# A four-layer graph network: L0's table in a written order with gathers ahead of its branch, and its one-hot columns on ScalarE

## Chip, cores and metric

One core of a Trainium2 chip runs the whole program in one launch. The metric is device time in microseconds (us), the median over runs. The engines are PE (TensorE: matmuls and transposes), DVE (VectorE), ACT (ScalarE), POOL (GpSimd, which issues the indirect DMAs) and SP (SyncE, which issues most other DMAs). Each engine works through its own queue of instructions in order and waits on semaphores that the others raise.

## What is computed

The input is a graph of 6250 nodes with 256 features and 100 000 edges sorted by destination. Four layers follow each other, each as `x = x + layer(relu(layernorm(x)))`. Only the first, L0, is touched; the part of it that matters is:

```python
h = jnp.maximum(_layernorm(x, axis=-1), 0.0)
Qh = (h @ Wq + bq).reshape(N, 8, 32)
Kh = (h @ Wk + bk).reshape(N, 8, 32)
Vh = (h @ Wv + bv).reshape(N, 8, 32)
s = jnp.einsum('nhc,nhc->nh', Qh, Kh) / jnp.sqrt(32.)
alpha = jax.nn.leaky_relu(s[src] + s[dst], 0.2)      # edges and self loops
e = jnp.exp(alpha - segment_max(alpha, dst)[dst])
a = e / segment_sum(e, dst)[dst]
attn = segment_sum(Vh[src] * a[:, :, None], dst).reshape(N, 256)
...
```

After it come a projection, a batch norm, a feed-forward part of width 512 and a second batch norm. L1 is a filter convolution, L2 an attention with edge features, L3 a graph convolution.

## The kernel before

The nodes are padded to 6272, which is NB = 49 blocks of 128. The edges are cut into G = 98 groups of J x 128 = 1024; since they are sorted by destination, the edges of one group reach at most 128 neighbouring nodes, a window that starts 64 nodes further on for each group.

**The table (L187 to L229).** For every block of nodes the kernel normalises the rows (`norm_stats`, `norm_t`), turns them with TensorE, multiplies them with Wq and Wk (into the buffer `ps_Q`) and with Wv (into `ps_V`), and forms the node's score per head on VectorE (L221 to L224). Bias terms of the score are folded into eight more columns of Wv (L194 to L206). A row of 265 numbers, which are V, the 8 scores and a one, is put together (L226 to L228) and stored to the table `vt` in DRAM by SP (L229). The order on each engine in this part is found by a scheduler from priorities; it is not written by hand. The x rows come by seven loads of seven blocks each, all issued by ScalarE at the start (L84 to L89).

**The checks and the branch (L232 to L271).** `first` (an iota on POOL) is the first node of each group's window. `rel` is each edge's destination within it. Minimum and maximum of `rel`, and a bound on the logits, become one flag, which every engine loads: a branch chooses between the fast path described here and a general one, which is not taken with these inputs.

**The edge loop of L0 (L755 to L791)** has its order written by hand, group by group. For group g:

- POOL gathers 8 x 128 rows of `vt` by `src` into one of six ring buffers in `xbuf` (L131, called at L765). A ring buffer comes free when the sums of the group six earlier are done.
- SP loads `drow`, the destinations of group g+2, to all partitions (L686, three buffers), and for a finished block b its own rows `v` (L769).
- `one_hot_t` (L692) makes the one-hot matrix `to` of group g+1 with nodes on partitions. VectorE compares `drow` with `place`, the node number of each partition in group g's window (an iota on POOL, L679). `to` has two buffers.
- `of_dst` (L706): 16 small products fetch each edge's destination score with `to`; `logits0` adds source and destination score and takes the exponential twice on ScalarE (L717 into `ps_E`, L718 into the gathered rows), and VectorE weights the rows (L780).
- `sum_window` (L630): eight products with `oh`, the one-hot matrix with edges on partitions (L698), sum the rows by destination. ScalarE copies the sums out (L632).
- Every second group a block of nodes is complete: `sum_block` (L640), `attn0` (L724 to L729), `turn0` (L735, L737), `project0` (L743) and `residual0` (L751, L753).

In the loop's text `logits0(g)` stands ahead of `one_hot_t(g + 1)`. The two matrices and the loop's order are these lines:

```python
nc.vector.tensor_scalar(tos[g], drows[g], place[:, g:g + 1], None, OP.is_equal)   # L692
...
nc.scalar.activation(ex, al, AF.Exp)                                              # L717
nc.scalar.activation(vg[:, :, D:D + H], al, AF.Exp)                               # L718
...
ex = logits0(g)                                                                   # L777
one_hot_t(g + 1)                                                                  # L778
```

Of the kernel before, what the change touches and what calls it, by code (L numbers as in the profile page):

```python
# [10 lines left out]
F32 = mybir.dt.float32  # L11
I32 = mybir.dt.int32
AF = mybir.ActivationFunctionType
# [22 lines left out]
def tile_gnn(ctx: ExitStack, tc: tile.TileContext, a: dict, out: bass.AP, N: int):  # L36
# [46 lines left out]

    def load_x():  # L84
        for b0 in range(0, NB, 7):
            b1 = min(NB, b0 + 7)
            nc.scalar.dma_start(x[:, b0:b1, :], xv[:, b0:b1, :])

    load_x()  # L89
    src_i = keep.tile([P, GJ], I32, name="src_i")  # L90
# [87 lines left out]

    vt = dram.tile([NP, VR], F32, name="vt")
    sct = dram.tile([NP, 2 * H], F32, name="sct")  # L180
    with ExitStack() as l0:
# [3 lines left out]
        wqk = wp.tile([P, 2, 2 * D], F32, name="wqk")  # L185
        wv = wp.tile([P, 2, D + H], F32, name="wv")
        nc.sync.dma_start(wqk[:, :, 0:D], a["L0_gnn_Wq"].rearrange("(c p) n -> p c n", p=P))  # L187
        nc.sync.dma_start(wqk[:, :, D:2 * D], a["L0_gnn_Wk"].rearrange("(c p) n -> p c n", p=P))
        nc.sync.dma_start(wv[:, :, 0:D], a["L0_gnn_Wv"].rearrange("(c p) n -> p c n", p=P))
        bq, bk = on_all(wp, "L0_gnn_bq", D), on_all(wp, "L0_gnn_bk", D)  # L190
        nc.sync.dma_start(src_i, a["src"])
        nc.sync.dma_start(dst_i, a["dst"])
        isq = 1.0 / math.sqrt(HD)
        nc.vector.tensor_scalar(wqk[:, :, 0:D], wqk[:, :, 0:D], isq, None, OP.mult)  # L194
        nc.vector.tensor_scalar(bq, bq, isq, None, OP.mult)
        both = wp.tile([P, 2, D], F32, name="both")
        other = wp.tile([P, 2, D], F32, name="other")
        nc.vector.tensor_tensor(both, wqk[:, :, 0:D], bk[:, None, :].to_broadcast([P, 2, D]), OP.mult)
        nc.vector.tensor_tensor(other, wqk[:, :, D:2 * D], bq[:, None, :].to_broadcast([P, 2, D]), OP.mult)
        nc.vector.tensor_tensor(both, both, other, OP.add)  # L200
        for k in range(2):
            nc.vector.tensor_reduce(wv[:, k, D:D + H], both[:, k, :].rearrange("p (h c) -> p h c", c=HD),
                                    AX.X, OP.add)
        bqk = wp.tile([P, H, 1], F32, name="bqk")
        nc.vector.tensor_tensor(bq, bq, bk, OP.mult)
        nc.vector.tensor_reduce(bqk[:, :, 0], bq.rearrange("p (h c) -> p h c", c=HD), AX.X, OP.add)  # L206

        with tc.tile_pool(name="a0", bufs=2) as ap:
            for b in range(NB):
                if b % 7 == 0:  # L210
                    norm_stats(b, min(NB, b + 7))
                hb = ht[:, :, b * P:(b + 1) * P]
                norm_t(ps, "T", ap, b, hb)
                qk, v = ps("Q", [P, 2 * D]), ps("V", [P, D + H])
                for k in range(2):
                    nc.tensor.matmul(qk, hb[:, k, :], wqk[:, k, :], start=k == 0, stop=k == 1)  # L216
                    nc.tensor.matmul(v, hb[:, k, :], wv[:, k, :], start=k == 0, stop=k == 1)
                q = ap.tile([P, D], F32, name="q")
                nc.scalar.activation(q, qk[:, 0:D], AF.Copy)
                qq = ap.tile([P, H, HD + 1], F32, name="qq")  # L220
                nc.vector.tensor_tensor(qq[:, :, 0:HD], q.rearrange("p (h c) -> p h c", c=HD),  # L221
                                        qk[:, D:2 * D].rearrange("p (h c) -> p h c", c=HD), OP.mult)
                nc.vector.tensor_tensor(qq[:, :, HD:HD + 1], bqk, v[:, D:D + H][:, :, None], OP.add)
                nc.vector.tensor_reduce(sv[:, b, :], qq, AX.X, OP.add)  # L224
                row = ap.tile([P, VR], F32, name="row", bufs=3)
                nc.scalar.activation(row[:, 0:D], v[:, 0:D], AF.Copy)  # L226
                nc.gpsimd.tensor_copy(row[:, D:D + H], sv[:, b, :])
                nc.gpsimd.memset(row[:, D + H:VR], 1.0)  # L228
                nc.sync.dma_start(vt[b * P:(b + 1) * P, :], row)  # L229


        bad = small.tile([P, 4], F32, name="bad")  # L232
        with tc.tile_pool(name="prep", bufs=1) as prep:
            first = prep.tile([P, G, J], F32, name="first")
            nc.gpsimd.iota(first, pattern=[[HW, G], [0, J]], base=-OFF, channel_multiplier=0,
                           allow_small_or_imprecise_dtypes=True)
            nc.vector.tensor_copy(rel, dst_i)
            rel3 = rel.rearrange("p (g j) -> p g j", j=J)
            nc.vector.tensor_tensor(rel3, rel3, first, OP.subtract)
            nc.vector.tensor_reduce(bad[:, 0:1], rel, AX.X, OP.min)  # L240
            nc.vector.tensor_scalar(bad[:, 0:1], bad[:, 0:1], -1.0, None, OP.mult)
            nc.vector.tensor_reduce(bad[:, 1:2], rel, AX.X, OP.max)
            nc.vector.tensor_scalar(bad[:, 1:2], bad[:, 1:2], P - 1.0, None, OP.subtract)

# [360 lines left out]
    def fast():  # L605
# [43 lines left out]


        l0 = fctx.enter_context(ExitStack())
# [6 lines left out]
        w1, w2 = next(of1), next(of2)  # L658
        NV = 2 * NACC // (J * VR)
        vgs = [xbuf[:, i * J * VR:(i + 1) * J * VR].rearrange("p (j r) -> p j r", j=J) for i in range(NV)]  # L660
        with tc.tile_pool(name="e0", bufs=2) as ep:

            scw = ep.tile([P, NB, 2, 2 * H], F32, name="scw", bufs=1)
            for odd in range(2):
                for b0, b1 in ((0, 32), (32, NB)):
                    t = ps("AB"[odd], [P, b1 - b0, 2 * H])
                    if odd:
                        b2 = min(b1, NB - 1)
                        nc.tensor.matmul(t, shift_by(-OFF), sc[:, b0:b1, :], start=True, stop=False)
                        nc.tensor.matmul(t[:, 0:b2 - b0, :], shift_by(P - OFF), sc[:, b0 + 1:b2 + 1, :],  # L670
                                         start=False, stop=True)
                    else:
                        b2 = max(b0, 1)
                        nc.tensor.matmul(t, shift_by(OFF), sc[:, b0:b1, :], start=True, stop=False)
                        nc.tensor.matmul(t[:, b2 - b0:, :], shift_by(OFF - P), sc[:, b2 - 1:b1 - 1, :],
                                         start=False, stop=True)
                    nc.vector.tensor_copy(scw[:, b0:b1, odd, :], t)
            place = ep.tile([P, G], F32, name="place", bufs=1)
            nc.gpsimd.iota(place, pattern=[[HW, G]], base=-OFF, channel_multiplier=1,  # L679
                           allow_small_or_imprecise_dtypes=True)  # L680
# [7 lines left out]
            def one_hot_t(g):  # L688

                if g < G:  # L690
                    tos[g] = ep.tile([P, J * P], F32, name="to")
                    nc.vector.tensor_scalar(tos[g], drows[g], place[:, g:g + 1], None, OP.is_equal)  # L692

# [15 lines left out]
            def logits0(g):  # L709

                vg, dg = vgs[g % NV], dgs[g]
                al = ep.tile([P, J, H], F32, name="al")
# [42 lines left out]
            with tc.manual_schedule():  # L755
# [5 lines left out]
                for g in range(G + 2):  # L761
                    vg = vgs[g % NV]
                    if g < G:
                        for j in range(J):
                            gather(vg[:, j, :], vt, src_i[:, g * J:(g + 1) * J], j)  # L765
                    loads0(g + 2)
# [8 lines left out]
                    projected = [(b, project0(b)) for b in blocks_done(g - 2)]  # L775
                    if g < G:
                        ex = logits0(g)  # L777
                        one_hot_t(g + 1)  # L778
                        vals = vg[:, :, 0:D].rearrange("p j (h c) -> p j h c", c=HD)
                        nc.vector.tensor_tensor(vals, vals, ex[:, :, :, None].to_broadcast([P, J, H, HD]),  # L780
                                                OP.mult)
# [14 lines left out]
        with tc.tile_pool(name="f0", bufs=2) as fp, Psum("psf", A=3, B=3, T=2) as ps:  # L796
            load_x()
            ff = l0.enter_context(tc.tile_pool(name="ff", bufs=1, side="right"))
# [328 lines left out]
    def slow():  # L1127
# [126 lines left out]
        with tc.tile_pool(name="f0", bufs=1) as fp:  # L1254
# [6 lines left out]
            for b in range(NB):  # L1261
# [7 lines left out]
                for o in range(2):  # L1269
# [6 lines left out]
                    nc.vector.bn_stats(st1[:, o, b, :], ht[:, o, b * P:b * P + n])  # L1276
            load_x()
            rs, sh = feed_forward(wp, fp, ps, w0, st1)
# [189 lines left out]
```

## Time and profile before

| | |
|---|---|
| median of three runs | 5322.65 us (5315.94 to 5338.24) |
| profiled execution: own time, span | 5275.56 us, 5273.8 us |
| mean granted TensorE clock | 0.747 |
| PE, PEld busy | 59%, 46% of the span |
| DVE, ACT, POOL busy | 39%, 11%, 58% |
| DMA traffic | 536.82 MB, mean 102 GB/s |

The first stages within the span, as the instructions' start times show them: L0's table to about 182 us, the checks and the branch to 193 us (first gather at 193.05), L0's edge loop to about 1394 us, L0's feed-forward part to about 1550 us. L1 follows to about 2730, L2 to about 4000 and L3 to the end.

How busy the engines are in the stages that the change touches, from the view of windows (start and end; length; busy time and instructions of PE, PEld, DVE, ACT and POOL; granted clock; DMA share; GB/s):

```profile
0.00:182.00 182.00, 146.93 (x490) 85.44 (x491) 83.38 (x315) 54.17 (x155) 15.40 (x109) 1.00 0.25 82
182.00:192.00 10.00, 0.86 (x3) 0.29 (x3) 8.15 (x19) 0.38 (x1) 2.10 (x2) 0.66 0.04 14
193.00:358.00 165.00, 95.93 (x364) 77.68 (x363) 58.67 (x157) 11.44 (x30) 101.42 (x105) 0.65 0.51 147
358.00:1347.00 989.00, 785.56 (x3457) 660.85 (x3455) 533.66 (x1472) 75.26 (x294) 657.84 (x672) 0.79 0.49 143
```

A row of the instruction groups reads: line, engine, operation, what it writes and reads, how often; its busy time in us and the mean of one in ns; the idle time of its engine just before it, and what ended most of that. In the waits view the numbers are us in total, times, and the longest. "remote" and "issue" stand for waits whose end the records do not explain by an instruction of this core, and for time in which the engine waited for nothing that the profile shows.

### The profile page before, as it was taken

How to read it: one execution, taken by the hardware profiler on the slowest of the kernel's cores; microseconds unless marked ns; L12 is line 12 of the kernel's file. 1: busy time of each engine (PE TensorE's matmuls, PEld its weight loads, DVE VectorE, ACT ScalarE, POOL GpSimd, SP SyncE). 2: the span in 40 equal slices, each digit the busy share in tenths (PEclk: the TensorE clock that was granted, in tenths of full speed). 3: DMA queues.
4: the chain of work that ended last, by engine and by line, in shares of the span. 5: the costliest groups of instructions: out<-in, count | busy, mean ns of one | idle time of the engine just before them, and what ended most of it. 6: DMA issues, size and time to landing. Idle time of an engine off the chain costs nothing.

```text
span 5273.8 us, 42603 instructions
## 1 busy us (share of the span) xinstructions
PE 3126.5 (59%) x12132; PEld 2420.0 (46%) x12133; DVE 2067.2 (39%) x6350; ACT 601.7 (11%) x1517; POOL 3046.8 (58%) x3261
## 2 busy tenths in 40 slices
PE   7577878778895154544544545555555355554645
PEld 4366766667545143333333434444444244443434
DVE  4355555555525155555555523233333122222212
ACT  2100000000133000000000012222222100000000
POOL 0456666666104665565665266666666466666665
PEclk9778777787897577677667777777777677776777
DMA  2344544445302233333333233333333233333332
GB/s 96 115 127 143 149 140 143 140 142 149 97 0 63 60 99 97 103 103 96 98 100 100 76 98 99 98 99 99 101 100 100 74 93 102 97 98 98 98 98 84
DMA packets 258746, 536.82 MB, mean 102 GB/s; under 512 B 65096, under 2 KB 144966, under 8 KB 258502
## 3 DMA queue, kind: packets, MB, share of 16 engines
q0 software_dynamic: 137984, 364.28, 25.8%
q1 hardware_dynamic: 107750, 156.85, 9.4%
q10 hardware_dynamic: 12768, 12.85, 0.8%
q8 instruction: 104, 1.70, 0.1%
q14 instruction: 140, 1.15, 0.1%
HBM read 504.57 MB, written 29.15 MB: 101 GB/s over the span
## 4 chain that ended last, share of the span: by engine, by line
PE 35%; another core or an unknown queue 26%; issue 16%; DVE 11%; ACT 5%; POOL 4%; DMA 1%; DVEq 0%; SPq 0%; ACTq 0%; POOLq 0%
PE ps_S L630 12%; PE ps_S L1118 5%; POOL vg L131 4%; PE ps_A L706 4%; DVE oh L932 3%; PE ps_T L640 3%; DVE big L969 2%; PE ps_Q L216 2%; PE ps_A L401 2%; PE ps_B L407 2%; DVE ea L974 2%; PE ps_B L743 1%; DVE te L975 1%; PE ps_S L972 1%
## 5 line engine op out<-in xcount | busy, mean ns | idle before, releaser
L131 POOL DMA_INDIRECT vg<-xt,src_i x1568 | 1490.6, 951 | 870.7 <-issue 542.2
L131 POOL DMA_INDIRECT big<-ht,src_i x784 | 742.0, 946 | 475.2 <-PE ps_S L972 215.9
L131 POOL DMA_INDIRECT xbuf<-vt,src_i x784 | 767.5, 979 | 397.6 <-issue 180.4
L630 PE MATMUL ps_S<-vg,oh 128*128 128x258 f32 x1568 | 476.0, 470 | 467.6 <-DVE oh L1039 455.5
L630 PEld LDWEIGHTS ps_S<-vg,oh 128*128 128x128 f32 x1568 | 373.7, 242 | 554.1 <-DVE oh L1039 467.4
L640 PE MATMUL ps_T<-ws,shifts 128*128 128x265 f32 (+2 forms) x1164 | 358.9, 441 | 388.2 <-issue 304.4
L1118 PE MATMUL ps_S<-vg,oh 128*128 128x256 f32 x1568 | 440.9, 438 | 167.3 <-issue 139.8
L630 PE MATMUL ps_S<-xbuf,oh 128*128 128x265 f32 x1568 | 491.1, 471 | 40.5 <-issue 38.0
L1039 DVE TENSOR_SCALAR oh<-iota,rel,ex 128x128 f32<-128x128 f32 x784 | 210.4, 360 | 694.3 <-ACT ex L1036 519.0
L640 PEld LDWEIGHTS ps_T<-ws,shifts 128*128 128x128 f32 x1164 | 243.0, 215 | 497.9 <-issue 377.7
L1118 PEld LDWEIGHTS ps_S<-vg,oh 128*128 128x128 f32 x1568 | 356.8, 228 | 227.9 <-issue 160.8
L630 PEld LDWEIGHTS ps_S<-xbuf,oh 128*128 128x128 f32 x1568 | 362.2, 237 | 126.2 <-issue 47.4
L972 PE MATMUL ps_S<-oh,big 128*128 128x128 f32 x1568 | 294.1, 362 | 185.5 <-issue 141.1
L1094 DVE TENSOR_SCALAR oh<-iota,rel 128x128 f32<-128x128 f32 x784 | 163.2, 297 | 584.9 <-remote 370.4
L972 PEld LDWEIGHTS ps_S<-oh,big 128*128 128x128 f32 x1568 | 281.2, 272 | 214.0 <-issue 155.9
L958 PE MATMUL ps_B<-wout,agg 128*128 128x256 f32 x98 | 55.8, 671 | 498.8 <-DVE agg L999 310.6
L780 DVE TENSOR_TENSOR xbuf<-xbuf,ps_E 128x2048 f32<-128x2048 f32 x98 | 223.8, 2284 | 238.0 <-issue 142.8
L706 PEld LDWEIGHTS ps_A<-scw,to 128*128 128x128 f32 x1568 | 258.1, 254 | 50.8 <-DVE to L692 23.2
L706 PE MATMUL ps_A<-scw,to 128*128 128x16 f32 x1568 | 251.8, 306 | 44.7 <-DVE to L692 32.1
L632 ACT ACTIVATE ws<-ps_S 128x265 f32<-128x265 f32 (+1 forms) x196 | 76.5, 390 | 1721.2 <-PE ps_S L630 833.0
L958 PEld LDWEIGHTS ps_B<-wout,agg 128*128 128x128 f32 x98 | 23.5, 298 | 517.0 <-issue 429.0
L924 PE MATMUL ps_A<-wr,rb 99*128 99x384 f32 (+1 forms) x588 | 211.3, 500 | 9.4 <-DMA rb<-in_rbf 9.4
(229 smaller groups left out, 3442.9 us busy)
## 6 DMA issues: line engine op xcount, KB each, us to landing
drow<-in_dst_row SPq DMA_DIRECT2D x98, 512.0 KB
ea<-in_edge_attr SPq DMA_DIRECT2D x98, 512.0 KB
vg<-xt,src_i POOLq DMA_INDIRECT x1568
xbuf<-in_x ACTq DMA_DIRECT2D x14, 896.0 KB
xbuf<-vt,src_i POOLq DMA_INDIRECT x784
big<-ht,src_i POOLq DMA_INDIRECT x784
rb<-in_rbf SPq DMA_DIRECT2D x196, 49.5 KB
vt<-row SPq DMA_DIRECT2D x49, 132.5 KB
```

Of the source, the lines that this page charges most:

```text
L131: nc.gpsimd.indirect_dma_start(out=rows, out_offset=None, in_=table, in_offset=bass.IndirectOffsetOnAxis(ap=idx[:, j:j + 1], axis=0))
L216: nc.tensor.matmul(qk, hb[:, k, :], wqk[:, k, :], start=k == 0, stop=k == 1)
L630: nc.tensor.matmul(s, oh[:, j, :], rows[:, j, :], start=j == 0, stop=j == J - 1)
L640: nc.tensor.matmul(t, shift_by(s), sums[g], start=i == 0, stop=i == len(parts) - 1)
L706: nc.tensor.matmul(dgs[g][:, j, :], tos[g][:, j * P:(j + 1) * P], scw[:, g // 2, g % 2, :], start=True, stop=True)
L780: nc.vector.tensor_tensor(vals, vals, ex[:, :, :, None].to_broadcast([P, J, H, HD]), OP.mult)
L924: nc.tensor.matmul(t, rbs[g][0:33 * n, g % 2, q, :], wr3[0:33 * n, 0:n, :], start=True, stop=True)
L932: nc.vector.tensor_scalar(ohs[g][:, j, :], iota, rel[:, c], w1["cut"][:, c], OP.is_equal, OP.mult)
L972: nc.tensor.matmul(s, hg[:, j, :], ohs[g][:, j, :], start=j == 0, stop=j == J - 1)
L1039: nc.vector.tensor_scalar(oh[:, j, :], iota, rel[:, g * J + j:g * J + j + 1], ex[:, j:j + 1], OP.is_equal, OP.mult)
L1094: nc.vector.tensor_scalar(oh[:, j, :], iota, rel[:, g * J + j:g * J + j + 1], None, OP.is_equal)
L1118: nc.tensor.matmul(s, oh[:, J - 1 - j, :], vg[:, J - 1 - j, :], start=j == 0, stop=j == J - 1)
```

## The change

- The loads of x are cut at blocks 0, 2, 8, 16, 24, 32, 40, 49 at the first use, and as before later. The loads of the two bias vectors stand ahead of the weights on SP.
- The table is written under a fixed order, with the blocks staggered (`normed0(b + 2)`, `turned_0(b + 1)`, `row0(b)`). The statistics' root is taken block by block. Both products of Q, then both of V. Wq is not scaled any more; the factor goes into the copy of q and into the score terms. The row buffers are three fixed tiles with their ones set once; the sum is written to the row, and POOL copies it to `sv`.
- `first` is made at the start, and the six operations on `rel` are interleaved with the blocks 3, 7, 11, 15, 19 and 23.
- The gathers of groups 0 to 3 (32 indirect DMAs) are issued after the table and ahead of the branch; the loop issues those from group 4 on.
- `one_hot_t` is two passes of ScalarE, `to = |drow + place|` with `place` negated, and `to = relu(1 - to)`. It stands ahead of `logits0(g)` in the loop's order.

```diff
+    load_x([0, 2, 8, 16, 24, 32, 40, NB])
...
+    AHEAD = 4
+    def rows0(g):
+        for j in range(J):
+            gather(vrows[g % NV][:, j, :], vt, src_i[:, g * J:(g + 1) * J], j)
...
+        def normed0(b):
+            if b < NB:
+                norm_stats(b, b + 1)
+                xns[b] = ap.tile([P, D], F32, name="xn")
+                nc.vector.tensor_scalar(xns[b], x[:, b, :], mv[:, b, 0:1], rstd[:, b, :],
+                                        OP.subtract, OP.mult)
...
+        def row0(b):
+            qk, v = ps("Q", [P, 2 * D]), ps("V", [P, D + H])
+            for k in range(2):
+                nc.tensor.matmul(qk, hbs[b][:, k, :], wqk[:, k, :], start=k == 0, stop=k == 1)
+            for k in range(2):
+                nc.tensor.matmul(v, hbs[b][:, k, :], wv[:, k, :], start=k == 0, stop=k == 1)
+            q = ap.tile([P, D], F32, name="q")
+            nc.scalar.activation(q, qk[:, 0:D], AF.Copy, scale=isq)
...
+            nc.vector.tensor_reduce(row[:, D:D + H], qq, AX.X, OP.add)
+            nc.gpsimd.tensor_copy(sv[:, b, :], row[:, D:D + H])
+            nc.sync.dma_start(vt[b * P:(b + 1) * P, :], row)
...
+        l0.enter_context(tc.manual_schedule())
+        normed0(0)
+        score_terms()
+        normed0(1)
+        turned_0(0)
+        for b in range(NB):
+            normed0(b + 2)
+            turned_0(b + 1)
+            row0(b)
+            if b % 4 == 3 and checks:
+                checks.pop(0)()
+        for g in range(AHEAD):
+            rows0(g)
...
-            nc.gpsimd.iota(place, pattern=[[HW, G]], base=-OFF, channel_multiplier=1,
+            nc.gpsimd.iota(place, pattern=[[-HW, G]], base=OFF, channel_multiplier=-1,
...
-                    nc.vector.tensor_scalar(tos[g], drows[g], place[:, g:g + 1], None, OP.is_equal)
+                    nc.scalar.activation(tos[g], drows[g], AF.Abs, bias=place[:, g:g + 1], scale=1.0)
+                    nc.scalar.activation(tos[g], tos[g], AF.Relu, bias=ones_c, scale=-1.0)
...
-                    if g < G:
-                        for j in range(J):
-                            gather(vg[:, j, :], vt, src_i[:, g * J:(g + 1) * J], j)
+                    if AHEAD <= g < G:
+                        rows0(g)
...
+                        one_hot_t(g + 1)
                         ex = logits0(g)
-                        one_hot_t(g + 1)
```

More of the change, by code (lines that the diff above doesn't have):

```diff
@@ L82, in tile_gnn, with load_x @@
     xv = a["x"].rearrange("(b p) d -> p b d", p=P)
-    def load_x():
-        for b0 in range(0, NB, 7):
-            b1 = min(NB, b0 + 7)
+    def load_x(ends):
+        for b0, b1 in zip(ends, ends[1:]):
             nc.scalar.dma_start(x[:, b0:b1, :], xv[:, b0:b1, :])
-    load_x()
+    load_x([0, 2, 8, 16, 24, 32, 40, NB])
     src_i = keep.tile([P, GJ], I32, name="src_i")
@@ L179, in tile_gnn @@
     vt = dram.tile([NP, VR], F32, name="vt")
+    NV = 2 * NACC // (J * VR)
+    AHEAD = 4
+    vrows = [xbuf[:, i * J * VR:(i + 1) * J * VR].rearrange("p (j r) -> p j r", j=J) for i in range(NV)]
+    def rows0(g):
+        for j in range(J):
+            gather(vrows[g % NV][:, j, :], vt, src_i[:, g * J:(g + 1) * J], j)
     sct = dram.tile([NP, 2 * H], F32, name="sct")
@@ L186, in tile_gnn @@
         wv = wp.tile([P, 2, D + H], F32, name="wv")
+        bq, bk = on_all(wp, "L0_gnn_bq", D), on_all(wp, "L0_gnn_bk", D)
         nc.sync.dma_start(wqk[:, :, 0:D], a["L0_gnn_Wq"].rearrange("(c p) n -> p c n", p=P))
@@ L189, in tile_gnn @@
         nc.sync.dma_start(wv[:, :, 0:D], a["L0_gnn_Wv"].rearrange("(c p) n -> p c n", p=P))
-        bq, bk = on_all(wp, "L0_gnn_bq", D), on_all(wp, "L0_gnn_bk", D)
         nc.sync.dma_start(src_i, a["src"])
@@ L193, in tile_gnn @@
         isq = 1.0 / math.sqrt(HD)
-        nc.vector.tensor_scalar(wqk[:, :, 0:D], wqk[:, :, 0:D], isq, None, OP.mult)
-        nc.vector.tensor_scalar(bq, bq, isq, None, OP.mult)
         both = wp.tile([P, 2, D], F32, name="both")
         other = wp.tile([P, 2, D], F32, name="other")
-        nc.vector.tensor_tensor(both, wqk[:, :, 0:D], bk[:, None, :].to_broadcast([P, 2, D]), OP.mult)
-        nc.vector.tensor_tensor(other, wqk[:, :, D:2 * D], bq[:, None, :].to_broadcast([P, 2, D]), OP.mult)
@@ L200, in tile_gnn @@
[L200 to L203, printed above, removed]
-        bqk = wp.tile([P, H, 1], F32, name="bqk")
[L205 to L214, printed above, removed]
-                for k in range(2):
[L216 to L229, printed above, removed]
@@ L232, in tile_gnn @@
[L232 to L243, printed above, removed]
+        bqk = wp.tile([P, H, 1], F32, name="bqk")
@@ new lines, in tile_gnn @@
+        rows = [wp.tile([P, VR], F32, name=f"row{i}") for i in range(3)]
+        for row in rows:
+            nc.gpsimd.memset(row[:, D + H:VR], 1.0)
+        first = wp.tile([P, G, J], F32, name="first")
+        nc.gpsimd.iota(first, pattern=[[HW, G], [0, J]], base=-OFF, channel_multiplier=0,
+                       allow_small_or_imprecise_dtypes=True)
+        bad = small.tile([P, 4], F32, name="bad")
+        ap = l0.enter_context(tc.tile_pool(name="a0", bufs=3))
+        xns, hbs = {}, {}
@@ new lines, in score_terms @@
+        def score_terms():
+            nc.vector.tensor_scalar(bq, bq, isq, None, OP.mult)
+            nc.vector.scalar_tensor_tensor(both, wqk[:, :, 0:D], isq, bk[:, None, :].to_broadcast([P, 2, D]),
+                                           op0=OP.mult, op1=OP.mult)
+            nc.vector.tensor_tensor(other, wqk[:, :, D:2 * D], bq[:, None, :].to_broadcast([P, 2, D]), OP.mult)
+            nc.vector.tensor_tensor(both, both, other, OP.add)
+            for k in range(2):
+                nc.vector.tensor_reduce(wv[:, k, D:D + H], both[:, k, :].rearrange("p (h c) -> p h c", c=HD),
+                                        AX.X, OP.add)
+            nc.vector.tensor_tensor(bq, bq, bk, OP.mult)
+            nc.vector.tensor_reduce(bqk[:, :, 0], bq.rearrange("p (h c) -> p h c", c=HD), AX.X, OP.add)
@@ new lines, in normed0, with turned_0 @@
+        def normed0(b):
[4 more added lines that the diff above has]
+                                        OP.subtract, OP.mult)
+        def turned_0(b):
+            if b < NB:
+                hbs[b] = ht[:, :, b * P:(b + 1) * P]
+                t = ps("T", [P, 2, P])
+                for k in range(2):
+                    nc.tensor.transpose(t[:, k, :], xns[b][:, k * P:(k + 1) * P], ident)
+                nc.scalar.activation(hbs[b], t, AF.Relu)
@@ new lines, in row0 @@
+        def row0(b):
+            qk, v = ps("Q", [P, 2 * D]), ps("V", [P, D + H])
+            for k in range(2):
+                nc.tensor.matmul(qk, hbs[b][:, k, :], wqk[:, k, :], start=k == 0, stop=k == 1)
+            for k in range(2):
+                nc.tensor.matmul(v, hbs[b][:, k, :], wv[:, k, :], start=k == 0, stop=k == 1)
+            q = ap.tile([P, D], F32, name="q")
+            nc.scalar.activation(q, qk[:, 0:D], AF.Copy, scale=isq)
+            qq = ap.tile([P, H, HD + 1], F32, name="qq")
+            nc.vector.tensor_tensor(qq[:, :, 0:HD], q.rearrange("p (h c) -> p h c", c=HD),
+                                    qk[:, D:2 * D].rearrange("p (h c) -> p h c", c=HD), OP.mult)
+            row = rows[b % 3]
+            nc.scalar.activation(row[:, 0:D], v[:, 0:D], AF.Copy)
+            nc.vector.tensor_tensor(qq[:, :, HD:HD + 1], bqk, v[:, D:D + H][:, :, None], OP.add)
+            nc.vector.tensor_reduce(row[:, D:D + H], qq, AX.X, OP.add)
+            nc.gpsimd.tensor_copy(sv[:, b, :], row[:, D:D + H])
+            nc.sync.dma_start(vt[b * P:(b + 1) * P, :], row)
@@ new lines, in tile_gnn @@
+        rel3 = rel.rearrange("p (g j) -> p g j", j=J)
+        checks = [lambda: nc.vector.tensor_copy(rel, dst_i),
+                  lambda: nc.vector.tensor_tensor(rel3, rel3, first, OP.subtract),
+                  lambda: nc.vector.tensor_reduce(bad[:, 0:1], rel, AX.X, OP.min),
+                  lambda: nc.vector.tensor_scalar(bad[:, 0:1], bad[:, 0:1], -1.0, None, OP.mult),
+                  lambda: nc.vector.tensor_reduce(bad[:, 1:2], rel, AX.X, OP.max),
+                  lambda: nc.vector.tensor_scalar(bad[:, 1:2], bad[:, 1:2], P - 1.0, None, OP.subtract)]
@@ L247, in tile_gnn @@
+        l0.enter_context(tc.manual_schedule())
[9 more added lines that the diff above has]
+                checks.pop(0)()
+        assert not checks
+        for g in range(AHEAD):
+            rows0(g)
         tmp = wp.tile([P, NB, H], F32, name="tmp")
@@ L658, in fast @@
         w1, w2 = next(of1), next(of2)
-        NV = 2 * NACC // (J * VR)
-        vgs = [xbuf[:, i * J * VR:(i + 1) * J * VR].rearrange("p (j r) -> p j r", j=J) for i in range(NV)]
         with tc.tile_pool(name="e0", bufs=2) as ep:
@@ L709, in logits0 @@
             def logits0(g):
-                vg, dg = vgs[g % NV], dgs[g]
+                vg, dg = vrows[g % NV], dgs[g]
                 al = ep.tile([P, J, H], F32, name="al")
@@ L761, in fast @@
                 for g in range(G + 2):
-                    vg = vgs[g % NV]
-                    if g < G:
-                        for j in range(J):
-                            gather(vg[:, j, :], vt, src_i[:, g * J:(g + 1) * J], j)
+                    vg = vrows[g % NV]
+                    if AHEAD <= g < G:
+                        rows0(g)
                     loads0(g + 2)
@@ L796, in fast @@
         with tc.tile_pool(name="f0", bufs=2) as fp, Psum("psf", A=3, B=3, T=2) as ps:
-            load_x()
+            load_x([*range(0, NB, 7), NB])
             ff = l0.enter_context(tc.tile_pool(name="ff", bufs=1, side="right"))
@@ L1276, in slow @@
                     nc.vector.bn_stats(st1[:, o, b, :], ht[:, o, b * P:b * P + n])
-            load_x()
+            load_x([*range(0, NB, 7), NB])
             rs, sh = feed_forward(wp, fp, ps, w0, st1)
```

## Prediction

> **What bounds the kernel now.** I read the engine rows first: PE 59% and POOL 58% of the span, DVE 39%, ACT 11%. No engine is full, so the question is who waits for whom, stage by stage. The edit touches two stages of the 5273.8 us: L0's table (0 to about 182 us) and L0's edge loop (first gather 193.05, last sums of group 97 near 1394). The rest keeps its program.
>
> In the edge loop the groups of instructions give the gathers' price: each of the 784 takes 0.979 us on POOL, and most have 0.30 us of issue ahead.
>
> ```profile
> L131 POOL DMA_INDIRECT xbuf<-vt,src_i x784 | 767.5, 979 | 397.6 <-issue 180.4
> ```
>
> So a group of eight costs POOL about 10.0 us and a pair of groups 20.0. But the pair's real period, counted over the gathers that start a group, is (1347.2 - 357.9) us / 42.5 pairs = 23.28 us: POOL also pauses. The waits of the stretch 300 to 1420 us say for what:
>
> ```profile
> ACT ws L632 <- PE ps_S L630: 501.8, 53, 11.8
> ACT ws L632 <- remote: 218.3, 18, 16.9
> POOL xbuf L131 <- issue: 159.4, 523, 0.3
> ...
> POOL xbuf L131 <- PE ps_S L630: 115.4, 94, 19.0
> ```
>
> The ring of six gathered groups is full, so POOL waits until the sums (L630) of six groups earlier are reported done; ScalarE, which copies the sums out (L632), is waiting most of the time. The timeline of one pair shows the order (start, length, engine, line):
>
> ```profile
> 898.80 1.29 POOL L131 DMA_INDIRECT xbuf<-vt,src_i  x1 [2.92 <-remote]
> ...
> 899.23 0.75 DVE L692 TENSOR_SCALAR to<-drow,place 128x1024 f32<-128x1024 int32 x1
> 899.42 0.23 ACT L717 ACTIVATE ps_E<-al 128x64 f32<-128x64 f32 x1
> ...
> 904.72 5.83 PE L630 MATMUL ps_S<-xbuf,oh 128*128 128x265 f32 x16
> ...
> 905.67 0.75 DVE L692 TENSOR_SCALAR to<-drow,place 128x1024 f32<-128x1024 int32 x1
> ...
> 911.11 0.39 ACT L632 ACTIVATE ws<-ps_S 128x265 f32<-128x265 f32 x1 [11.12 <-PE ps_S L630]
> 911.39 0.22 ACT L717 ACTIVATE ps_E<-al 128x64 f32<-128x64 f32 x1
> ```
>
> POOL stops once per pair for 2.92 us and restarts; from that restart exp, L780, 16 small products L706 and the sums follow, twice. This chain of compute adds to about 19.3 us; the rest of the 23.3 is completions that arrive late (the "remote" wait: sums of one group of each pair are marked done only when POOL has gone quiet). The loop is thus held by POOL and by these completions, with the compute chain some 4 us behind.
>
> **The change part by part.** The profiled execution is 0.9% under the median of the runs (5275.56 against 5322.65 us), so I work out differences from it and add them to the median.
>
> *Table.* Before, TensorE's work sets a cadence of 3.085 us per block (6.17 us per two) after a first Q product at 29.17. The new order sends a first x load of two blocks, but ScalarE still issues seven loads, and before it was busy with them from 0.78 to 18.83 us; its first square root comes behind that. I take the first Q 2 us earlier. DVE per block: statistics 0.39 + 0.17, reciprocal 0.18, normalising 0.41, products 0.42 + 0.16, sum 0.43 = 2.16; ScalarE: root 0.30, three copies of 0.38 = 1.44; the written order couples the two to about 2.95 per block beside TensorE's 2.9. Six check operations (up to 0.98 each, about 3.5 in all) now fall inside this cadence. 27 + 49 x 2.95 + 3.5 = 175, plus the tail of one block = about 178 against 182: -3 us, between -5 and +10 if the written order stalls where a scheduler would have slipped work in. The 49 ones settings on POOL (0.09 each) were hidden: nothing.
>
> *Checks and flag.* The iota `first` waited for POOL's copy of the last row and ran at 184.96 (1.51 us) with four checks behind it; flag written at 191.40. With both gone ahead, only the bound on the logits (L248 to L265) remains after the last row: flag 3 to 5 us earlier.
>
> *Gathers ahead.* The first 32 start once the last rows have landed (184.81 before): about 181.5 instead of 193.05, -11.5 us for POOL. But everything POOL issues after them is moved too: the flag's load, and the iota `place`, now stand behind 32 x 1.2525 = 40.1 us of gathers, so `place` comes at about 222.7 instead of 192.26. The first column one-hot needs it: about 224 instead of 216.9. SP's weight loads after the branch wait for nothing on POOL and come 3 to 5 us earlier. Ring space: 48 gathers fit, then POOL waits for S(0), at 247.84 before and between 235 and 251 after. Net gain at the start -5 to -17, taken -12.
>
> *One-hot columns on ScalarE.* DVE loses 0.755 us per group. ScalarE gets two passes over 1024 elements that the trace doesn't show; nearest rows:
>
> ```profile
> L395 ACT ACTIVATE hn<-big,sh,rs 128x512 f32<-128x512 f32 x24 | 18.1, 805 | 71.3 <-DVE big L409 70.4 <-DVE sh L382 1.0
> ...
> L470 ACT ACTIVATE cut<-te,halfpi 128x784 f32<-128x784 f32 x1 | 0.9, 947 | 0.0
> ```
>
> The widths 128 and 512 of the first operation (485 and 805 ns) differ by 0.833 ns per element; 947 + 240 x 0.833 = 1147 ns per pass, 2.3 us for two. They stand ahead of the two exponentials of L717/L718 on ScalarE, in order: exp(g), then L780, then the sums of g wait for them. In the even group of a pair exp would start 0.6 us after the restart and goes to about 3.1, L780 to 5.7, while TensorE is busy with L743 and L706 until 6.1: covered, +0.2 at most. In the odd group the Abs can't begin before ws of the even group (911.11 above), exp goes from 911.4 to 913.7 and its sums from 914.0 to 916.4: uncovered, +2.35 on the compute chain, 19.3 to 21.9 with both. `drow` comes free later too, after the Abs behind ws instead of the 905.67 one, which shifts the next row load on SP by about 7 us; it is needed only two groups on, so its data aren't late; behind it on SP stands the `v` load of the next finished block, which L724 needs about one group later: hidden too.
>
> What that is worth in the period: if POOL and the completions keep setting 23.28, nothing (lower end); if all of it shows, 2.35 x 49 = +115 us (upper end). The nearest row is in the trace itself: three stretches (709 to 782, 922 to 997, 1067 to 1138) where POOL pauses in both groups of a pair because both sums finish close to the time that POOL needs their space. There nine pairs take 217.8 us, 24.2 each; the other 33.5 average 23.03. A later S(odd) is just what brings a pair into this kind: +1.17 for the other 36 of some 45 pairs = +42 us. After the last gather (1357.6) groups 93 to 97 run at the bare chain of 7.2 us: there nothing hides the passes, and less 0.75 for DVE they cost about 1.6 each, +8. Before the ring fills the same shows in a few groups: +4.
>
> *What leaves DVE frees POOL.* The Trainium skill (SBUF — State Buffer, Who interferes with whom) says that a vector operation in its two-port mode, which `tensor_scalar` can enter, locks GpSimd out for the whole instruction, so that descriptors of gathers aren't written. It speaks for this edit: L692 is such an operation, and by the rule its going frees up to 98 x 0.755 = 74 us of POOL. The row says less: the 109 gathers that overlap an L692 take 1.137 us, the 526 that overlap neither it nor L698 0.948. The trace agrees in kind, not in size: 109 x 0.19 = 21 us, 0.43 per pair. Where a pause follows anyway, POOL only waits longer; I credit half, -10.
>
> A rule against the edit is in TensorE: Matmul & The Clock Gate, Part 1: an idle window of some 3.4 us puts TensorE at half clock. In the windows view the granted clock around S(even) and S(odd) is
>
> ```profile
> 904.60:910.60 6.00, 6.00 (x19) 4.80 (x19) 1.63 (x5) 0.00 (x0) 4.48 (x6) 0.65 0.67 203
> ...
> 914.00:917.20 3.20, 3.18 (x13) 2.19 (x12) 0.00 (x0) 0.00 (x0) 2.29 (x4) 1.00 0.36 97
> ```
>
> (clock third from the end: 0.65, then 1.00), and S takes 5.83 us in the first, 3.83 in warm odd groups. The new gap ahead of S(odd) is 2.35 us, shorter than the rule's window, so by the rule alone the clock may hold: 0. If it drops, 2.0 x 49 = +98, in the slow rival.
>
> Sum: -12 start, +42 two-pause pairs, +4 and +8 bare chain, -10 gathers = **+32 us**: 5322.65 + 32 = 5355 us. Own spread 5330 to 5395.
>
> **Rivals.**
> *Hidden (no change).* The odd groups' 2.35 stays below POOL and the completions: -12 + 4 + 8, and gathers -21 to 0: 5302 to 5323. For: the chain has 4 us of margin. Against: S(odd) is released late in most pairs, so what it gains in margin may already be spent. Chance 0.22.
> *Faster.* The late completions themselves go. In the trace the held copies of sums (over 0.5 us after S; 50 of 98) had a median of 0 KB of SP's loads in the 2 us before, the 48 unheld ones 291 KB. The row load shifts from about 7 us to about 15 us after the restart, next to S(odd). If it releases the odd sums in every pair, the period falls to the chain, 21.9: -1.38 x 45 = -62, with -12 + 12 at the ends and lighter gathers up to -21: 5240 to 5262. It decides once ws(odd) starts within 0.5 us of its sums. Against: a correlation is no cause. Chance 0.20.
> *Much slower.* The same shift takes the load away from S(even), whose completions then hang, or the gap ahead of S(odd) halves the clock: chain and pauses add, +2.35 to +4 per pair: +115 to +170, 5437 to 5490. Chance 0.13.
> *The edit doesn't do what it says.* If POOL's loads of the flag hold other engines at the branch until the 32 gathers are over, the -12 turns into up to +30; inside the main case's range.
>
> **How the numbers follow.** Main case 0.45, hidden 0.22, faster 0.20, much slower 0.13. A measurement of this kernel tells about 0.5% (27 us) from no change. Slower: 0.40 of the main case and 0.13; same: 0.05 and 0.16; faster: 0.06 and 0.20. Range 5250 to 5440: the faster and much slower rivals' nearer halves are in, some 0.15 is left out.
>
> **What would show it.** Right: two ScalarE groups of 98 with about 1.15 us each; gathers' mean near 0.95; first gather near 181 and `place` near 223; exp(odd) 2.3 us later after ws(even); POOL's pauses on both groups of most pairs; layers 1 to 3 unchanged. Wrong: a pair period under 23 us, S(even) over 6 us, or a first column one-hot that doesn't wait for `place`.

## The result, and the profile after

The changed kernel takes 5346.57 us (median of 8 runs, 5334.49 to 5358.91) against 5322.52 us (8 runs, 5315.94 to 5338.98): a ratio of 1.0042, 95% interval 1.0030 to 1.0054. That is 24 us slower; the forecast was 5355, 32 us slower. The move is clear of the scatter, but inside the 0.5% that the forecast called no change.

The rows of the instruction groups: the sums in the kernel before, then gathers and sums in the changed kernel (its own line numbers: the gathers are L130, the sums L670):

```profile
L630 PE MATMUL ps_S<-xbuf,oh 128*128 128x265 f32 x1568 | 491.1, 471 | 40.5 <-issue 38.0
```

```profile
L130 POOL DMA_INDIRECT xbuf<-vt,src_i x784 | 743.9, 949 | 460.2 <-PE ps_S L670 264.9
...
L670 PE MATMUL ps_S<-xbuf,oh 128*128 128x265 f32 x1568 | 564.2, 535 | 64.1 <-issue 64.0
```

A gather takes 949 ns instead of 979, as long as those took before that met neither one-hot matrix on VectorE (948). A product of the sums takes 535 ns instead of the 471 of before (477 and 474 in two later traces of that kernel). The operation, its operands and its number are the same. This row is the one that the forecast didn't have in its main case.

ScalarE's groups by shape, in the stretch 300 to 1450 us:

```profile
L732 ACT ACTIVATE to<-to,ones_c 128x1024 f32<-128x1024 f32 x92 | 105.5, 1147 | 3.0
L731 ACT ACTIVATE to<-drow,place 128x1024 f32<-128x1024 int32 x92 | 105.1, 1143 | 0.0
```

Each pass takes what the two nearest rows gave (1147 ns). The timeline of POOL at the start:

```profile
180.60 1.13 POOL L130 DMA_INDIRECT xbuf<-vt,src_i  x1 [2.73 <-DMA vt<-row]
...
219.61 0.95 POOL L130 DMA_INDIRECT xbuf<-vt,src_i  x1 [0.30 <-issue]
220.58 0.24 POOL L717 IOTA place<- 128x98 f32 x1
220.98 0.96 POOL L130 DMA_INDIRECT xbuf<-vt,src_i  x1 [0.16 <-issue]
```

Gathers run from 180.60, and `place` has to wait for all 32 of them. The waits of the stretch 300 to 1420 us (us in total, times, longest):

```profile
ACT ws L672 <- PE ps_S L670: 643.0, 78, 9.7
POOL xbuf L130 <- PE ps_S L670: 243.7, 173, 17.9
...
ACT ws L672 <- remote: 175.3, 13, 15.0
```

POOL's wait for sums rose from 115.4 us (165.0 and 170.7 in the two later traces of the kernel before, see below) to 243.7 us. It now pauses over 1 us at 78 of 86 starts of a group, before at 48 (57 and 52).

### The profile page after: what moved, and what is told of

It reads as the page before. It is cut to its first block, busy times and chain, and to the rows that moved or that the text cites. A ratio compares the mean times of both kernels' runs of the same rounds, so it can differ in the third digit from the quotient of the medians.

```text
span 5342.8 us, 42689 instructions
## 1 busy us (share of the span) xinstructions
PE 3130.6 (59%) x12132; PEld 2406.4 (45%) x12133; DVE 2024.3 (38%) x6293; ACT 818.2 (15%) x1755; POOL 3019.0 (57%) x3215
## 5 line engine op out<-in xcount | busy, mean ns | idle before, releaser
L130 POOL DMA_INDIRECT vg<-xt,src_i x1568 | 1490.2, 950 | 890.6 <-issue 545.7
L130 POOL DMA_INDIRECT big<-ht,src_i x784 | 741.9, 946 | 481.4 <-PE ps_S L1011 191.7
L130 POOL DMA_INDIRECT xbuf<-vt,src_i x784 | 743.9, 949 | 460.2 <-PE ps_S L670 264.9
L670 PE MATMUL ps_S<-vg,oh 128*128 128x258 f32 x1568 | 474.6, 469 | 428.9 <-DVE oh L1078 415.1
L670 PEld LDWEIGHTS ps_S<-vg,oh 128*128 128x128 f32 x1568 | 372.8, 242 | 517.8 <-DVE oh L1078 429.9
L670 PE MATMUL ps_S<-xbuf,oh 128*128 128x265 f32 x1568 | 564.2, 535 | 64.1 <-issue 64.0
L680 PE MATMUL ps_T<-ws,shifts 128*128 128x265 f32 (+2 forms) x1164 | 338.1, 433 | 372.9 <-issue 226.7
L670 PEld LDWEIGHTS ps_S<-xbuf,oh 128*128 128x128 f32 x1568 | 420.4, 275 | 176.8 <-issue 70.3
L746 PE MATMUL ps_A<-scw,to 128*128 128x16 f32 x1568 | 219.4, 283 | 109.3 <-ACT to L732 67.8
L746 PEld LDWEIGHTS ps_A<-scw,to 128*128 128x128 f32 x1568 | 209.8, 215 | 140.4 <-ACT to L732 84.8
```

The costliest lines, as they stand in the source:

```text
L130: nc.gpsimd.indirect_dma_start(out=rows, out_offset=None, in_=table, in_offset=bass.IndirectOffsetOnAxis(ap=idx[:, j:j + 1], axis=0))
L670: nc.tensor.matmul(s, oh[:, j, :], rows[:, j, :], start=j == 0, stop=j == J - 1)
L680: nc.tensor.matmul(t, shift_by(s), sums[g], start=i == 0, stop=i == len(parts) - 1)
L746: nc.tensor.matmul(dgs[g][:, j, :], tos[g][:, j * P:(j + 1) * P], scw[:, g // 2, g % 2, :], start=True, stop=True)
```

## The experiments

The profiled execution of the kernel before turned out to be a quick one (5275.56 us). So times of single traces are set against two more traces of the same kernel, and effects are read from ratios wherever these exist. The experiments ran in three groups of four, each group on one chip. Two chips, called kind A here, ran the kernel before in about 5324 us, like the first measurement; the chip of the second group, B, ran it in 4512.7 us. Each chip was used in one group of runs only.

Two counts are used below, both over groups 14 to 91, which are 78. The sums of a group are called late when ScalarE's copy of them starts more than 0.5 us after their end in the trace (the ends of TensorE's products are modelled there), and at full clock when they take under 4.5 us, mostly 3.83.

**1. The kernel before again.**

> The kernel before, unchanged, for a second trace. The first one's execution took 5275.56 us, 47 us under the median of its kind; this one should take about 5322 us. If the first trace is typical of L0, the sums of group 97 end near 1394 us and the difference lies in layers 1 to 3; if it is not, they end some 20 to 40 us later and the loop's pair period is over 23.3 us.

5319.21 us. The sums of group 97 end at 1414.39 us instead of 1394.08, and a pair takes 23.95 us instead of 23.53, counted from gather to gather of groups 14 to 96. The first trace is at the low end of its kind in L0, and in the later layers too, where the rest of its 43.6 us lies. A third trace (experiment 12) has 24.22 us per pair. A difference of two single traces under some 0.7 us per pair means nothing.

**2. The table alone, and 3. the columns alone.**

```diff
 # 2: the changed kernel, with
-                    nc.scalar.activation(tos[g], drows[g], AF.Abs, bias=place[:, g:g + 1], scale=1.0)
-                    nc.scalar.activation(tos[g], tos[g], AF.Relu, bias=ones_c, scale=-1.0)
+                    nc.vector.tensor_scalar(tos[g], drows[g], place[:, g:g + 1], None, OP.is_equal)
...
+                        ex = logits0(g)
                         one_hot_t(g + 1)
-                        ex = logits0(g)
```

(with the sign of `place` as before). Number 3 is the kernel before with the opposite edits and nothing else.

> The table and the gathers ahead of the branch as changed; the one-hot columns on VectorE (is_equal) behind logits0, as before. Theory A (the columns on ScalarE cost, the table brings a little): 5310 to 5323 us, 0 to 12 us under the kernel before; the first column one-hot still waits for place at about 220 us, so the gathers ahead bring POOL 7 us at the 49th gather and the sums of group 0 nothing. Rival B (the early part is what costs): 5335 to 5347 us, as the changed kernel.

> The kernel before with only the one-hot columns on ScalarE and ahead of logits0. Theory A: 5340 to 5360 us, the whole loss of the changed kernel and some more; POOL pauses in both groups of most pairs and the stretch after the last gather is longer by 23 us (59.9 against 36.5). Rival B: 5322 us within its spread.

Table alone: 5317.56 us, ratio 0.9980 (0.9967 to 0.9994). Columns alone: 5349.66 us, ratio 1.0053 (1.0036 to 1.0069). Theory A holds, rival B falls: the table gains 0.2%, the columns lose 0.5%, and the two add up to the change (1.0042 in the first measurement). The columns' trace ends the sums of group 97 at 1446.41, 32.0 us after experiment 1's (23 were expected behind the last gather alone); 16.2 of that is there at the last gather, the rest in the groups behind it. A pair takes 24.52 us there, and 24.25 in the trace of the table alone, which has the loop of before.

Those last groups have no gather beside them and show the cost bare. The windows view of that stretch, first the kernel before in experiment 1, then the changed kernel (length; busy time of PE, PEld, DVE, ACT, POOL; granted clock; DMA share; GB/s):

```profile
1379.00:1414.00 35.00, 32.46 (x183) 27.72 (x182) 28.63 (x77) 3.83 (x17) 0.00 (x0) 1.00 0.50 154
```

```profile
1391.00:1442.00 51.00, 43.00 (x190) 34.70 (x189) 26.01 (x72) 12.72 (x25) 0.00 (x0) 0.83 0.33 106
```

The clock was 1.00 throughout and is now 0.83 on the average. (After the last gather it is 1.00 in the first trace of before too and 0.91 in the third, where TensorE runs at half for 4.6 us at its beginning and 3.41 us in its middle without the new gaps.) The timelines of PE, in experiment 1 and then in the changed kernel, show what happens:

```profile
1387.59 1.86 PE L706 MATMUL ps_A<-scw,to 128*128 128x16 f32 x16
1389.30 3.83 PE L630 MATMUL ps_S<-xbuf,oh 128*128 128x265 f32 x16
1392.97 1.95 PE L640 MATMUL ps_T<-ws,shifts 128*128 128x265 f32 x8
1394.75 1.85 PE L706 MATMUL ps_A<-scw,to 128*128 128x16 f32 x16
```

```profile
1404.89 1.96 PE L746 MATMUL ps_A<-scw,to 128*128 128x16 f32 x16 [1.06 <-ACT to L732]
1407.37 5.42 PE L670 MATMUL ps_S<-xbuf,oh 128*128 128x265 f32 x16 [0.53 <-issue]
1412.63 1.95 PE L680 MATMUL ps_T<-ws,shifts 128*128 128x265 f32 x8
1415.49 1.96 PE L746 MATMUL ps_A<-scw,to 128*128 128x16 f32 x16 [0.91 <-ACT to L732]
1417.97 5.24 PE L670 MATMUL ps_S<-xbuf,oh 128*128 128x265 f32 x16 [0.52 <-issue]
```

TensorE waits about 1 us for the second pass (L732) ahead of the small products and 0.5 us behind them. The records of the granted clock then alternate between 6.83 us at full and 3.41 us at half, and the sums, which fall in the half, take 5.2 to 5.5 us instead of 3.83. A group takes 10.6 to 11.0 us against 7.2 before. Some 1.5 us of that are the longer sums; the rest, some 2 us, is what shows of the 2.3 us of passes, since TensorE itself had been the limit before. That the gaps bring the half clock is tested in number 6.

**4. The passes behind the exponentials.**

```diff
+                        ex = logits0(g)
                         one_hot_t(g + 1)
-                        ex = logits0(g)
```

> The changed kernel with one_hot_t(g + 1) behind logits0(g), so that the two passes of ScalarE stand behind the two exponentials. If the loss is that exp and the weighting of the rows wait 2.3 us behind the passes, this takes it back: the stretch after the last gather falls from 59.9 towards 40 us and the time to about 5315 to 5330 us. If instead the 16 small products of the next group need the matrix earlier than ScalarE can give it, they now wait (the matrix comes 0.5 us later still) and the time stays at 5345 us or rises to 5360.

5401.91 us, ratio 1.0147 (1.0124 to 1.0170): worse than either branch of the expectation, and in kind the second. In TensorE's order the small products of g+1 (L746) stand ahead of the sums of g. With the passes behind exp these products begin 2.7 us after exp, and the sums 4.5 us after exp (median) instead of 2.6: they wait for the matrix instead. The order in the changed kernel is the better of the two. Whether it hurts that the passes for group g+1 are made in group g at all is what the next experiment tests.

**5. The columns one group earlier.**

```diff
                 one_hot_t(0)
+                one_hot_t(1)
...
-                    loads0(g + 2)
+                    loads0(g + 3)
...
-                        one_hot_t(g + 1)
                         ex = logits0(g)
...
+                    one_hot_t(g + 2)
                     of_dst(g + 1)
```

> The changed kernel with the columns of group g+2 instead of g+1 made by ScalarE in group g, behind the two exponentials, and the row loads one group earlier; same number of operations and bytes. Theory A (the two passes cost because exp(g), or the next group's small products, wait for them, and because TensorE's clock falls in the gap): nothing waits now, the stretch after the last gather goes back from 60 to about 37 us, the sums to 3.83 us there, and the time to 5310 to 5325 us. Rival C (late completions of TensorE's sums set the pair, whatever ScalarE does): the loop stays at 24.3 us per pair and only the last stretch gets shorter: about 5325 us. Rival D (ScalarE's own 2.3 us per group, or its traffic, costs): no gain, 5345 us.

**6. Two idle products in the gap.**

```diff
+                    st = ps("S", [P, VR]) if g < G else None
+                    for _ in range(2 if g < G else 0):
+                        nc.tensor.matmul(st, ident, shifts[:, 0:VR], start=True, stop=True)
                     of_dst(g + 1)
...
-                        sums[g] = sum_window(ep, ohs[g], vg, VR)
+                        sums[g] = sum_window(ep, ohs[g], vg, VR, st)
```

> The changed kernel with two idle products (identity by constants, into the bank that the group's sums then overwrite) on TensorE ahead of the 16 small products of each group, in the gap where it waits for ScalarE. If the half clock in that gap is a cost of its own, the sums go from 5.5 to 3.83 us after the last gather, that stretch from 60 to about 53 us, and the loop gets shorter by up to 1.5 us per group that isn't held: 5300 to 5340 us. If sums at full clock are only reported late (in the second trace of the kernel before 25 of some 31 sums of 3.8 us were held, and few of the slow ones), the stretch after the last gather is shorter but the loop isn't, or is longer: 5335 to 5360 us.

**7. `place` first, and 8. the same with the table alone.** Both move the iota `place` among the constants at the start; number 8 does it to experiment 2's kernel.

> The changed kernel with the iota `place` made at the start, ahead of the gathers. Theory A: the first column one-hot no longer waits until 220 us; it follows the branch at about 190 us, the sums of group 0 end some 10 to 20 us earlier than 258 us, and the time falls by 5 to 12 us: 5335 to 5342. If the flag's load on POOL, which also stands behind the gathers, holds the other engines at the branch, nothing changes.

> The table and the gathers ahead as changed, the columns on VectorE as before, and `place` made at the start: 5305 to 5312 us, that is another 5 to 12 us under the run with the table alone.

These four ran on chip B, where the kernel before takes 4512.72 us:

| run | us | ratio (95%) | us per pair | sums over 0.5 us late |
|---|---|---|---|---|
| 5 group earlier | 4463.54 | 0.9890 (0.9875 to 0.9906) | 20.12 | 0 |
| 6 gap filled | 4527.33 | 1.0031 (1.0019 to 1.0044) | 20.49 | 0 |
| 7 `place` first | 4591.76 | 1.0176 (1.0162 to 1.0189) | 22.07 | 0 |
| 8 table, `place` first | 4500.65 | 0.9968 (0.9956 to 0.9980) | 20.91 | 0 |

On this chip no sums are late; on the chips of kind A 40 to 42 of 78 are in the three traces of the kernel before. Here the columns' cost stands bare: number 7 takes 2.0% more than number 8. The windows view 450 to 1150 us of 7, 6 and 5, in this order:

```profile
450.00:1150.00 700.00, 591.55 (x2586) 478.28 (x2585) 356.39 (x1043) 189.45 (x346) 477.57 (x504) 0.81 0.51 152
```

```profile
450.00:1150.00 700.00, 639.54 (x3088) 521.74 (x3088) 387.21 (x1123) 206.97 (x378) 519.97 (x548) 0.89 0.56 165
```

```profile
450.00:1150.00 700.00, 593.21 (x2864) 499.58 (x2863) 395.03 (x1141) 220.96 (x381) 530.43 (x557) 0.84 0.57 168
```

In the same 700 us POOL gets through 504 operations in 7, 548 in 6 and 557 in 5 (POOL's count, the fifth number in brackets). Two useless products per group raise the clock from 0.81 to 0.89, the mean time of a group's sums falls from 5.77 to 4.92 us, and a pair is 1.58 us shorter, 20.49 instead of 22.07. Over 41 pairs that is 65 us, the whole difference between the two runs (64.4). The two differ in `place` too, but its effect is seen apart: with `place` first the sums of group 0 end at 225.2 us instead of 237.5, and still gather 49 starts at 241.4 instead of 240.8. So the early columns bring POOL nothing at the 49th gather: it was not waiting for them. The expectations of 5 to 8 were made for a chip of the first kind, so their times can't be compared. What 7 and 8 expected of `place` itself, 5 to 12 us, can't be checked either, since the changed kernel and the table alone were not run on this chip; the start came as expected, and the 49th gather speaks against the gain.

With the columns made one group earlier (5) POOL pauses over 1 us at no start of a group and sets the pair alone: 16 gathers at 1.25 us are 20.0, measured 20.12. The stretch behind the last gather is 12.9 us, against 57.5 in number 7, since fewer groups are left there when POOL sets the pace. With the columns on VectorE (8) POOL sets the pair too, but gathers take 1001 ns in the loop instead of 953, and the pair 20.91. The rows of the gathers in 5 and 8, 300 to 1450 us:

```profile
L130 POOL DMA_INDIRECT xbuf<-vt,src_i x689 | 656.3, 953 | 209.9 <-issue 108.5 <-PE ps_S L670 60.9 <-DMA xbuf<-vt,src_i 14.9
```

```profile
L133 POOL DMA_INDIRECT xbuf<-vt,src_i x691 | 691.9, 1001 | 210.5 <-issue 89.3 <-PE ps_S L673 68.3 <-DMA xbuf<-vt,src_i 28.0
```

So rival D of number 5, that ScalarE's work as such costs, falls: with the same passes made earlier the kernel is 1.1% quicker than before. Number 5 also loads the rows of destinations one group earlier, which was not tried alone. Rival C concerns chips with late sums and is left to number 11.

**9 to 12. On the other chip of kind A.** Number 11 has the edits of 5 and 7 together.

> The changed kernel itself, beside the other three on one chip. The chip of the last four runs reports no sum late and ran the kernel before in 4512.7 us. Theory A (the passes open gaps in which TensorE's clock falls, and late sums had hidden it): on such a chip the loop is bound by the chain of compute, about 22 us per pair against POOL's 20.1 to 20.9, and the change costs 1.5 to 2%, some 4580 to 4600 us. On a chip that reports sums late it costs 0.4%, 5340 to 5350 us. Rival B (the loss is the same work on any chip): 0.4 to 0.5% on both.

> The changed kernel with two idle products in TensorE's gap, beside the changed kernel on the same chip. Theory A: on a chip without late sums 1.2 to 1.5% under the changed kernel (about 4527 against 4590 us), most of the loss, since the clock is worth more than the 2.3 us of passes. On a chip with late sums within 0.5% of it. Rival (the clock is no cost of its own, the passes are): no better than the changed kernel on either.

> The columns one group earlier on ScalarE, and `place` made at the start. Without late sums the loop is bound by POOL at 20.1 us per pair: about 1.1% under the kernel before, as the run without `place`, since the 49th gather starts no earlier for it. With late sums: 0.2 to 0.6% under the kernel before.

> The kernel before, for its trace on this chip. Without late sums: POOL issues without pauses, 20.9 us per pair with gathers of about 1.0 us where they meet the columns on VectorE, sums of group 97 within 45 us after the last gather. With late sums: 23.9 us per pair, as in the second trace.

| run | us | ratio (95%) | us per pair | sums at full clock, of 78 | all sums over 0.5 us late |
|---|---|---|---|---|---|
| 9 the change | 5338.81 | 1.0023 (1.0009 to 1.0036) | 24.38 | 0 | 10 |
| 10 gap filled | 5320.48 | 0.9989 (0.9970 to 1.0007) | 24.25 | 29 | 51 |
| 11 earlier, `place` first | 5323.58 | 1.0002 (0.9989 to 1.0016) | 23.74 | 38 | 47 |
| 12 before | 5329.05 | one run | 24.22 | 27 | 42 |

The change costs 0.2% here, less than the 0.4% first measured and expected; the intervals touch. Filling the gap takes it back, 18 us, and no more. The last two columns suggest why so little is to be had on such a chip. Sums at full clock are mostly reported late: 17 of 22, 22 of 30 and 23 of 27 in the three traces of the kernel before. In the changed kernel not one of 78 runs at full clock, and 10 or 11 are late, against 40 to 42. By these counts a slow sum that is reported at once is worth about as much as a quick one that is reported late. The clock is not the whole of it: of the slow sums, too, 37 to 43% were late before, 13 or 14% are in the changed kernel, and 59% (29 of 49) with the gap filled. No run separates the two. Number 5 gains 1.1% on chip B; number 11, the same with `place` first, gains nothing on kind A. The expected gain of 0.2 to 0.6% there was a miss. With 5323.58 us it doesn't tell theory A and rival C of number 5 apart on such a chip.

Where POOL sets the loop, number 5 (0.9890) is the quickest of the versions run; on kind A only the table alone (2) was measurably under the kernel before.

## Why the prediction came near

*The table and the start.* Forecast -12 us, the table alone measured 0.20% (-11 us by that ratio, -3 to -18). The pieces: table end 177.61 (forecast 178), first gather 180.60 (181.5), flag at 184.60, 6.9 us earlier (3 to 5), `place` at 220.58 (222.7), first columns at 220.85 (224). The sums of group 0 end at 258.4 us, as in experiments 1 and 12 (258.7, 259.9; 254.4 in the first trace), so the gathers ahead bring L0's chain of compute nothing at the start. Gather 49 comes 7 us earlier, not the assumed 12. Where the rest of the table's 11 us comes from, the traces don't settle: the trace of number 2 ends L0's loop 1.9 us later than experiment 1's, which is within their scatter.

*The passes.* 1147 ns forecast, 1147 and 1143 measured; exp behind them as said; pauses in both groups of nearly every pair, as said. That step was right in kind. Its size: forecast +42 for the pauses less 10 for the gathers. The two traces of the changed kernel have 24.35 and 24.38 us per pair, the three of before 23.53, 23.95 and 24.22: +0.47 on the average, some +19 us over 41 pairs where the forecast had +32, with a scatter of the same order.

*The last groups.* Forecast +8, since passes were to cost 1.6 us per group. The two traces of the changed kernel need 59.9 and 53.8 us after the last gather, the three of before 36.5, 37.9 and 44.1: +17 us. Here, and in the loop, a step failed: "by the rule alone the clock may hold: 0". It did not hold. No gap here had the rule's 3.4 us: gaps of 1.0 and 0.5 us in a group of 10.6 us went with the half clock, and filling the gap raised it (number 6). The rule decided for the wrong side because I read it as a threshold on one gap. The row that speaks is the clock itself, 1.00 in the last groups before and 0.83 after. In the sum the term should have been +1.5 us per group.

*Why the total came out near all the same.* In part this is luck: about 13 us too much for the loop and 9 too little for the last groups nearly cancel. With the table's -11 the measured parts, +19 and +17, add to +25. In the loop the mean granted clock hardly fell (0.79 to 0.78, and it is 0.78 in the third trace of before). The windows view 450 to 1150 us, before and after:

```profile
450.00:1150.00 700.00, 548.81 (x2435) 463.01 (x2433) 376.40 (x1034) 53.69 (x210) 464.11 (x475) 0.79 0.49 143
```

```profile
450.00:1150.00 700.00, 555.12 (x2360) 452.78 (x2360) 326.13 (x941) 174.54 (x318) 438.41 (x462) 0.78 0.47 139
```

But the half clock now falls on the sums of every group: their mean time goes from 5.12 to 5.47 us in the traces of before to 5.74 and 5.78 in those of the changed kernel. On chips of kind A this comes with the loss of a wait that was there: late sums fell from about 41 to 11 of 78. That is half of the rival called faster: the late completions did go. But nothing points to SP's row loads. In the second and third trace of before the sums that were not late also had a median of 0 KB of these loads in the 2 us before, so that correlation was an accident of one trace. And the gain was used up, as far as these counts tell, by the half clock, which the much slower rival had named. That the two nearly cancel here is argued from the counts, not shown by a run. On chip B, which has no late sums, the changed kernel itself was not run; with `place` first it loses 1.8%, so the much slower rival's sign and kind would be right there.

*POOL and VectorE.* POOL's pair was put at 20.0 us; its own row, 979 ns and 0.30 us of issue, gives 20.5, and number 8 measured 20.91. The sum credited 10 us for quicker gathers. On chip B, where POOL sets the loop, the columns on VectorE cost 0.79 us per pair (20.91 against 20.12), nearer to the row's 0.43 than to the rule's 98 x 0.755 = 74 us, which would be 1.5 per pair.

## What to carry to other kernels

An operation that is moved to an idle engine is free only if nothing waits for it in the same round of the loop: the two passes cost 0.5% (number 3, kind A) or 2.0% (7 against 8, chip B) when made one group ahead. Made two groups ahead in the same number of buffers, they left the time of the kernel before on kind A (number 11) and gained 0.8% on chip B (5 against 8). When a wait of TensorE is added, price the clock too: count all gaps in a few microseconds, not the longest one, and look at the time of the products that the rest waits for, since the mean clock of a stretch can stay the same while its half falls on them. And take more than one trace of the kernel before, on more than one chip if there is one, before a pattern of waits is made into a cause.

## What the runs showed of the hardware

The same program took 5324 us on two chips and 4512.7 us on another. In L0's loop the difference goes with completions of TensorE that are reported up to some 11 us late on kind A in the kernel before, most often those of sums at full clock, and in no trace of the other. In the last five groups, which have no gather beside them, they are in time on both. The later layers show the same in kind: the sums copied more than 0.5 us late are 48 of 98 in L2 and 74 to 85 of 98 in L3 in every trace of kind A, and one or none in those of chip B. In L1 the 784 gathers run over 1221 us in experiment 1 and 982 in number 8, at 944 and 948 ns each: POOL works as fast and pauses more. What holds the completions is open; the traffic of SP's queue goes with them in one trace of three, and no run here was made for it. In these records the granted clock is only ever 1.0 or 0.5 within L0's loop, in pieces of 3.41 us and multiples of that; two useless products in a gap of about 1 us kept more of these pieces at full (0.81 to 0.89), and on the chip without late sums made a pair 1.58 us shorter.
